# Two cross-attention layers on one core: the order of the second layer's heads, and its query channels with a batch in each of two PSUM banks

## The chip, the cores and the metric

The kernel runs on one core of a Trainium2 chip. The metric is the device time of one execution in microseconds (us), from the hardware's own clock; lower is better. The time before is the median of three runs. One further execution was profiled; durations of single instructions come from it.

## The reference

Two cross-attention layers follow each other. There are 64 batches of 256 tokens with 320 channels, and for each batch a context of 77 rows with 512 channels, of which the last 4 are image rows. All is fp32, with 20 heads of 16 channels. Cut to what matters:

```python
# layer 0                                  # layer 1
q = x @ Wq.T                               q = x1 @ W_q
p = softmax(q k^T / 4)     # 77 rows       p = softmax(q k_t^T / 4)    # 73 text rows
o = p v  (+ image part)                    t = p v_t
x1 = o @ Wo.T + bo + x                     sem = l2norm(p @ text) . l2norm(image rows)
                                           pi = softmax(q k_ip^T / 4 + 0.5 sem) * mask
                                           out = (t + pi v_ip) @ W_out + b_out + x1
```

Layer 1's input is layer 0's output, so layer 1 of a pair of batches can only start when layer 0 has finished with that pair.

## The kernel before, in words

Channels lie on partitions: 320 channels are two full tiles of 128 (`main`) and 64 left over (`last`). Two batches form a pair, and there are 32 pairs. The 64 left-over channels of a pair's first batch lie on partitions 0 to 63 and those of the second batch on partitions 64 to 127 of one tile, so `last` is a full 128-row tile with one batch in each half. The weights for it (`w[:, 2]` and `w[:, 3]`) have zeros in the other batch's half.

Heads go in three parts: part 0 and part 1 with eight heads each, part 2 with the last four. A unit is eight head-and-token-tile combinations: for parts 0 and 1 one half (128 tokens) of a batch's tokens, for part 2 four heads with both halves at once. `UNITS` lists the five units of a batch, so that a pair has `NU` = 10 units in each layer.

The main loop runs over blocks `g`; `p, k = divmod(g, NU)`, so ten blocks (k = 0 to 9) make a round. Block `g` handles unit `g` of layer 0 and unit `g - LAG` of layer 1, with `LAG` = 13: layer 1 of a pair begins in block 3 of the next round. In a block, in this order:

- TensorE computes into one four-bank tile `sc`: `semantics` of an earlier layer-1 unit (L762, L768), `scores` of layer 0, `scores` of layer 1 (L648).
- VectorE takes the maximum and subtracts it for both layers (`shifted`, L666 and L668), then multiplies the semantics with the probabilities (`weighted`, L779 and L782).
- TensorE transposes layer 1's probabilities of the previous block (`transposed`, L712 and L713), which ScalarE copies out (L719). ScalarE does layer 0's exponential (L676).
- Then comes the list `first` of extra steps, layer 0's transposes (L712; copies L738 and L739), `sums_out` (ScalarE, L1093), layer 1's exponential (L679, L680), `normalize` (L694, L695 on VectorE, L699 on POOL), what `later` holds, the list `second`, `attend` (L795, L800) and the list `third`.

`fillers(k, p)` says which extra steps stand in which block: projections of queries, keys and values, output projections, placing of values, and so on. The order on each engine is the order in which the program writes them (`keep_order`), so a waiting instruction holds all that is behind it on its engine.

PSUM has eight banks: four for `sc` (a single buffer), two for `ptr` (tag `tr`) and two for `pms` (tag `ms`). The next block's first matmul into `sc` needs this block's readers of it to be done, `sums_out` last.

The steps around the change:

- `queries(l, p, m)` makes query channels in one bank. For m = 0 and 1 it uses two matmuls of 512 columns over `main` (L562) and two of 256 columns over `last` (L564), whose stationary operand is 128 rows deep with one half zero; a copy (L565) follows. For m = 2, the last four heads, it uses four matmuls over `main` (L570) and four over `last` (L577), and a copy (L582).
- `halves(name, w, src)` makes 256 output channels with one batch in each of two banks: eight matmuls of 256 columns over `main` (L535), and later, in `rest()`, four over `last` (L544) that are 64 rows deep: batch 0 on rows 0 to 63, batch 1 on rows 64 to 127. `first_queries` uses it for layer 0's parts 0 and 1, and `project` for the output projections. Their ends are kept in `held` and are written at the start of the next block: the matmuls L544, then the drains (L593 on ScalarE for queries, four additions L608 on VectorE for a projection).
- `project_last` makes the last 64 output channels (L623) and adds them to the input tile (L627 on VectorE). After `project(0, p)` and `project_last(0, p)`, the input tile of pair `p` holds layer 1's input.
- The image attention of a batch runs through several blocks. Its exponential L925 (ScalarE) is in `later` of block 1 or 6, and `image_weights` (L932, L933 on VectorE) is in `early` of the next block, ahead of the drains.

Of the kernel before, what the change touches and what calls it, by code (L numbers as in the profile page):

```python
# [8 lines left out]
F32 = mybir.dt.float32  # L9
# [7 lines left out]
C = 320  # L17
E = 512
S = 256
# [3 lines left out]
P = 128  # L23
# [3 lines left out]
HALF = 64  # L27
# [4 lines left out]
QR = 32  # L32
SLOTS = H + 4

UNITS = ((0, 0), (0, 1), (1, 0), (1, 1), (2, 0))

PLACES = (0, 24, 8, 32, 16)
HT = H - 4
NU = 2 * len(UNITS)
LAG = NU + 3  # L40
SCALE = D**-0.5
SEM = 0.5
# [21 lines left out]
def tile_two_cross_attentions(ctx: ExitStack, tc: tile.TileContext, a: dict, out: bass.AP):  # L64
# [35 lines left out]
    nc = tc.nc  # L100
    x_in, c_in, cip_in = a["x"], a["ctx"], a["ctx_ip"]
    NB = x_in.shape[1] // S
    NP = NB // 2
    S2 = 2 * S
# [45 lines left out]
    cts, xts = {}, {}  # L150
# [400 lines left out]

    held = {}

    def queries(l, p, m):

        main, last = xts[p]
        ps = pms.tile([P, 512], F32, tag="ms", name=f"q_ps{l}_{p}_{m}")
        if m < 2:
            q = qs[l, p, m] = big.tile([P, S2], F32, tag=f"q{l}{m}", name=f"q{l}_{p}_{m}", bufs=1)
            c = slice(m * P, (m + 1) * P)  # L560
            for i in range(2):
                nc.tensor.matmul(ps, wq[l][:, i, c], main[:, i, :], start=(i == 0), stop=False)  # L562
            for b in range(2):
                nc.tensor.matmul(ps[:, b * S : (b + 1) * S], wq[l][:, 2 + b, c], last, start=False, stop=(b == 1))  # L564
            nc.scalar.copy(q, ps)  # L565
            return
        to = [ps[s * HALF : (s + 1) * HALF, :S].rearrange("p (b t) -> p b t", b=2) for s in range(2)]
        for i in range(2):
            for s in range(2):
                nc.tensor.matmul(  # L570
                    to[s], wq[l][:, i, C - HALF :],
                    main[:, i, :].rearrange("p (b s t) -> p b s t", b=2, s=2)[:, :, s, :],
                    start=(i == 0), stop=False,
                )
        for b in range(2):
            for s in range(2):
                nc.tensor.matmul(  # L577
                    to[s][:, b, :], wq[l][:, 2 + b, C - HALF :], last[:, s * P : (s + 1) * P],
                    start=False, stop=(b == 1),
                )  # L580
        q = qs[l, p, 2] = big.tile([P, 2, P], F32, tag=f"q{l}2", name=f"q{l}_{p}_2", bufs=1)
        nc.scalar.copy(q.rearrange("p b t -> p (b t)"), ps[:, :S])  # L582

    def first_queries(p):

        rest = halves(f"q_ps0_{p}", wq[0], xts[p])

        def end():
            ps = rest()
            q = big.tile([P, 2, S2], F32, tag="q0", name=f"q0_{p}")  # L590
            for m in range(2):
                qs[0, p, m] = q[:, m, :]
            return [lambda b=b: nc.scalar.copy(q[:, :, b * S : (b + 1) * S], ps[b]) for b in range(2)]  # L593

        held["q"] = end
# [45 lines left out]

    def scores(ps, start, stop, l, p, b, u):

        part, s = UNITS[u]
        q, kbd, t0 = qs[l, p, part], kbds[l, b], b * S + s * P
        for r in range(4):
            rows = slice(r * QR, (r + 1) * QR)
            nc.tensor.matmul(  # L648
                ps[:, r, 2 * T * l : 2 * T * (l + 1)], q[rows, b, :] if part == 2 else q[rows, t0 : t0 + P],
                kbd[rows, part].rearrange("p e t -> p (e t)"), start=start, stop=stop,  # L650
            )
# [52 lines left out]
    def transposed(l, p, b, u, w):  # L704

        n = P if l else 8 * R0
        part, s = UNITS[u]
        flat = w.rearrange("p i j t -> p (i j t)") if l else w
        ps = ptr.tile([P, 4, P], F32, tag="tr", name=f"tr{l}_{p}_{b}{u}")
        pr = ptr.tile([P, 4, P], F32, tag="tr", name=f"rtr{l}_{p}_{b}{u}")  # L710
        for i in range(4):
            nc.tensor.transpose(ps[:, i, :], flat[:, i * P : (i + 1) * P], ident)  # L712
        nc.tensor.transpose(pr[:n, 0, :], flat[:, 4 * P : 4 * P + n], ident)  # L713
        if l:
            pts[1] = (
                sp.tile([P, 4, P], F32, tag="pt1", name=f"pt1_{p}_{b}_{u}"),
                sp.tile([n, P], F32, tag="pr1", name=f"pr1_{p}_{b}_{u}"),
            )
            nc.scalar.copy(pts[1][0], ps)  # L719
            nc.scalar.copy(pts[1][1], pr[:n, 0, :])  # L720
            return
        if part == 2:
            pt, rt = pts[0, 2, b] = (
                sp.tile([P, 2, S], F32, tag="pt2", name=f"pt2_{p}_{b}"),
                sp.tile([n, P], F32, tag="pr2", name=f"pr2_{p}_{b}"),
            )
            nc.scalar.copy(
                pt.rearrange("p l (s t) -> p s l t", s=2), ps.rearrange("p (s l) t -> p s l t", s=2)
            )
            nc.scalar.copy(rt, pr[:n, 0, :])  # L730
            return
        if s == 0:
            pts[0, part] = (
                sp.tile([P, 4, S], F32, tag="pt0", name=f"pt0_{p}_{b}_{part}"),
                sp.tile([n, S], F32, tag="pr0", name=f"pr0_{p}_{b}_{part}"),
            )
        pt, rt = pts[0, part]
        nc.scalar.copy(pt[:, :, s * P : (s + 1) * P], ps)  # L738
        nc.scalar.copy(rt[:, s * P : (s + 1) * P], pr[:n, 0, :])  # L739
# [12 lines left out]
    def semantics(ps, start, stop, p, b, u, rows):  # L752

        part, _ = UNITS[u]
        pt, rt = rows
        for i in range(4):
            for j in range(2):
                half_rows = slice(j * M, (j + 1) * M)  # L760
                at = SEM0 + i // 2 * GV
                nc.tensor.matmul(  # L762
                    ps[:, i % 2 * 2 + j, at : at + GV], pt[half_rows, i, :], gv[b][half_rows, part, i, :],
                    start=start and i < 2, stop=False,
                )
        for r in range(4):
            quarter = slice(r * QR, (r + 1) * QR)
            nc.tensor.matmul(  # L768
                ps[:, r, SEM0 : SEM0 + 2 * GV].rearrange("p (e d) -> p e d", d=GV)[:, :, M:],
                rt[quarter, :], gr[b][quarter, part], start=False, stop=stop,  # L770
            )
# [13 lines left out]
    def attend(p, b, part):  # L785
# [2 lines left out]
        if (0, p) not in aTs:  # L788
            aTs[0, p] = channels("aT0", f"aT0_{p}", 1)
        main, last = aTs[0, p]  # L790
        ps = pms.tile([P, 2, S], F32, tag="ms", name=f"pv{p}_{b}_{part}")
        both = b == 1 and part == 1

        def heads(to, b, pair, pt, start):
# [186 lines left out]
    def fillers(k, p):  # L981
# [4 lines left out]
        def add(half, q, fn, *args):  # L986
            if 0 <= q < NP:
                f[half].append((fn, args))
# [12 lines left out]
        elif k == 1:  # L1001
            if p == 0:
                for l in range(2):
                    add(l, p, value_rows, 1, l)
                add(1, p, place_values, 0, p, 0)
            add(0, p, queries, 0, p, 2)
            add(1, p - 1, project, 0, p - 1)
            add(1, p - 2, last_image_values, p - 2, 0)
            add(1, p - 1, place_gram, 0)
            add(1, p, keys_by_head, 0, p, 1)  # L1010
# [1 line left out]
        elif k == 2:  # L1012
# [2 lines left out]
                    add(0, p, keys, 1, p, i)  # L1015
            add(0, p - 1, project_last, 0, p - 1)
            add(1, p + 1, load_x, p + 1)
            add(1, p - 1, queries, 1, p - 1, 0)
            add(1, p - 1, place_values, 1, p - 1, 0)
            add(1, p, values, 0, p, 1)  # L1020
        elif k == 3:
            add(0, p + 1, load_context, p + 1)
            add(0, p - 1, queries, 1, p - 1, 2)
            if p == 0:
                add(1, p, image_keys, 0)
            add(1, p - 1, queries, 1, p - 1, 1)
            add(1, p, place_values, 0, p, 1)
            add(1, p - 1, keys_by_head, 1, p - 1, 1)
        elif k == 4:
# [3 lines left out]
                add(0, p, keys, 1, p, 0)  # L1033
            add(1, p - 1, values, 1, p - 1, 1)
            add(1, p - 2, last_image_outputs, p - 2, 0)
            add(1, p + 1, first_queries, p + 1)
        elif k == 5:
            if p == 0:
                add(0, p, image_keys, 2)
# [39 lines left out]
    rows_todo, made_rows = [], [0, 1]  # L1079

    def unit(g):
        return (g // NU, g % NU // len(UNITS), g % len(UNITS)) if 0 <= g < NP * NU else None

    for i in range(2):
        keys(0, 0, i)
    last_keys(0)
    keys_by_head(0, 0, 0)
    first_queries(0)
    for fn in held.pop("q")():
        fn()  # L1090

# [7 lines left out]
    for g in range(NP * NU + LAG + 12):  # L1099
# [7 lines left out]
        for fn, args in early.pop(g, ()):  # L1107
            fn(*args)
        drains = [fn for what in ("q", "o") if what in held for fn in held.pop(what)()]
        if now[0] or now[1] or before1:  # L1110
            ps = psc.tile([P, 4, 512], F32, tag="sc", name=f"sc{g}")
            todo = []
            if before1:
                todo.append((semantics, (*before1[:3], before1[4])))
            for l in range(2):
                if now[l]:
                    todo.append((scores, (l, *now[l])))
            for n, (fn, args) in enumerate(todo):
                fn(ps, n == 0, n == len(todo) - 1, *args)
# [3 lines left out]
            drains += held.pop("i")()  # L1123
        for fn in drains:
            fn()
        ends = before1 and before1[2] == len(UNITS) - 1
        for l in range(2):
            if now[l]:
                shifted(ps, l, *now[l])
# [12 lines left out]
            keep_busy(6)  # L1142
        for fn, args in first:
            fn(*args)
        if before1 and k == 8:
            sums_out(ps)
        if last0:
            transposed(0, *last0)
# [6 lines left out]
            keep_busy(8)  # L1155
        if now[0] and k == 5:
            exponential(0, g, *now[0])
        if before1 and k != 8:
            sums_out(ps)
        if now[1]:  # L1160
            exponential(1, g, *now[1])
# [15 lines left out]
            fn(*args)  # L1177
        if last0:
            q, b, u, _ = last0
            if u == 1 or u == len(UNITS) - 1:  # L1180
                attend(q, b, int(u > 1))
        for fn, args in third:
            fn(*args)
# [58 lines left out]
```

## Time and profile before

| what | value |
|---|---|
| median of 3 runs | 2592.84 us (2590.41 to 2593.07) |
| the profiled execution | 2590.22 us |
| its span, first to last instruction | 2588.5 us |
| granted TensorE clock, mean | 0.998 |
| busy shares PE, DVE, ACT, POOL | 98%, 76%, 59%, 64% |
| first block with semantics starts | 113.05 us after the span's start |

Busy time is the time in which at least one instruction of an engine ran. PE is TensorE's matmuls, PEld its weight loads, DVE is VectorE, ACT is ScalarE, POOL is GpSimd. A busy share over the whole span is a mean over stages with different limits, so the stages that the change touches are read one by one, by the start times in the timeline. An arrow at the end of a timeline line names the idle time of the engine ahead of the group and who ended it.

### The profile page before, as it was taken

The numbers are of one execution on the slowest core, as the hardware profiler recorded it, in microseconds if no ns is written. First come the engines' busy times: TensorE is split into PE (matmuls) and PEld (weight loads), VectorE is DVE, ScalarE is ACT, GpSimd is POOL, SyncE is SP. The second block draws the span as 40 slices with busy tenths as digits, with TensorE's granted clock in tenths as the row PEclk, the third lists the DMA queues.
The fourth block names the chain that finished last, engine by engine and source line by source line (L and its number), as shares of the span: only waits on it lengthen the run. The fifth ranks groups of instructions, "written<-read, shape, count | busy, mean of one in ns | idle before, by whom it ended". The sixth has DMA issues, their size and how long they took to land.

```text
span 2588.5 us, 74021 instructions
## 1 busy us (share of the span) xinstructions
PE 2536.5 (98%) x26922; PEld 1977.1 (76%) x26922; DVE 1958.5 (76%) x3609; ACT 1520.3 (59%) x3893; POOL 1653.5 (64%) x4026
## 2 busy tenths in 40 slices
PE   7999999999999999999999999999999999999998
PEld 5677877777777777777777777777777777777676
DVE  4577777877777878777777777778777778777764
ACT  3465665665665665665665665665665665665543
POOL 3466666676666676666676666676666676666653
PEclk9999999999999999999999999999999999999999
DMA  5212211112211122211121211122211121211100
GB/s 165 59 44 59 65 45 44 51 54 60 62 47 48 47 59 55 62 45 49 48 59 55 62 45 50 47 59 54 64 44 50 45 60 54 62 40 40 27 25 26
DMA packets 186403, 138.29 MB, mean 53 GB/s; under 512 B 81017, under 2 KB 164729, under 8 KB 186041
## 3 DMA queue, kind: packets, MB, share of 16 engines
q1 hardware_dynamic: 185176, 132.41, 18.6%
q8 instruction: 215, 3.52, 0.6%
q14 instruction: 148, 1.20, 0.2%
q10 hardware_dynamic: 864, 1.15, 0.1%
HBM read 95.56 MB, written 33.91 MB: 50 GB/s over the span
## 4 chain that ended last, share of the span: by engine, by line
PE 89%; DVE 5%; ACT 2%; DMA 1%; POOL 1%; issue 1%; SPq 1%; DVEq 0%; ACTq 0%; POOLq 0%
PE sc L762 13%; PE tr L712 12%; PE o_ps L535 8%; PE sc L648 7%; PE sc L768 5%; PE v_ps L379 4%; PE q_ps L562 4%; PE q_ps L535 4%; PE k_ps L334 4%; PE o_ps L623 4%; PE pv L795 3%; PE o_ps L544 3%; PE pv L800 3%; PE q_ps L570 2%; PE rtr L713 2%; PE q_ps L564 2%
## 5 line engine op out<-in xcount | busy, mean ns | idle before, releaser
L666 DVE TENSOR_REDUCE mx<-sc 128x8 f32<-128x584 f32 (+1 forms) x640 | 497.5, 777 | 431.1 <-PE sc L648 431.0
L699 POOL TENSOR_TENSOR parts<-w,sm 128x512 f32<-128x512 f32 (+1 forms) x640 | 440.5, 710 | 372.3 <-DVE sm L695 163.7
L668 DVE TENSOR_TENSOR w<-sc,mx 128x616 f32<-128x616 f32 x640 | 512.0, 800 | 66.7 <-ACT kT L337 0.5
L719 ACT COPY pt<-tr 128x512 f32<-128x512 f32 x320 | 187.5, 586 | 466.4 <-PE tr L712 459.3
L712 PE MATMUL tr<-ident,parts 128*128 128x128 f32 x2560 | 410.1, 283 | 8.1 <-POOL parts L699 3.8
L762 PEld LDWEIGHTS sc<-gv,pt 64*128 64x128 f32 x5120 | 316.8, 187 | 88.2 <-ACT sums L1093 44.2
L712 PEld LDWEIGHTS tr<-ident,parts 128*128 128x128 f32 x2560 | 282.5, 141 | 117.8 <-issue 70.4
L762 PE MATMUL sc<-gv,pt 64*128 64x94 f32 x5120 | 356.3, 278 | 12.8 <-ACT sums L1093 10.4
L676 ACT ACTIVATE w<-w 128x616 f32<-128x616 f32 x320 | 231.0, 722 | 127.8 <-DVE w L668 119.2
L694 DVE TENSOR_REDUCE sm<-w 128x8 f32<-128x616 f32 x320 | 250.9, 784 | 14.4 <-ACT w L676 14.4
L648 PE MATMUL sc<-kbd,q 32*128 32x154 f32 x5120 | 247.6, 305 | 0.8 <-ACT q L593 0.8
L535 PE MATMUL o_ps<-aT,wo 128*128 128x256 f32 x1024 | 232.6, 380 | 0.0
L1168 DVE TENSOR_REDUCE nrm<-prod 128x8 f32<-128x584 f32 x320 | 227.0, 709 | 0.4
L779 DVE TENSOR_TENSOR prod<-sc,parts 128x512 f32<-128x512 f32 x320 | 217.9, 681 | 4.0 <-PE sc L768 4.0
L535 PEld LDWEIGHTS o_ps<-aT,wo 128*128 128x128 f32 x1024 | 190.4, 191 | 23.4
L679 ACT ACTIVATE parts<-w 128x512 f32<-128x512 f32 x320 | 206.9, 647 | 0.0
L738 ACT COPY pt<-tr 128x512 f32<-128x512 f32 x256 | 150.7, 589 | 69.7 <-PE tr L712 69.4
L648 PEld LDWEIGHTS sc<-kbd,q 32*128 32x128 f32 x5120 | 186.5, 186 | 5.4 <-issue 5.1
L1093 ACT COPY sums<-sc 128x168 f32<-128x168 f32 x320 | 96.6, 302 | 157.2 <-DVE prod L782 156.5
L683 POOL COPY att<-w 128x32 f32<-128x32 f32 x320 | 67.7, 212 | 186.9 <-DVE w L668 184.8
L379 PE MATMUL v_ps<-wv,cf 128*128 128x320 f32 (+1 forms) x624 | 182.1, 438 | 0.0
L713 PE MATMUL rtr<-ident,parts 128*104 128x128 f32 (+1 forms) x640 | 174.6, 273 | 0.0
(152 smaller groups left out, 4977.7 us busy)
## 6 DMA issues: line engine op xcount, KB each, us to landing
vip<-vip_rows SPq DMA_DIRECT2D x1024, 4.0 KB
out_dram<-x SPq DMA_DIRECT2D x64, 256.0 KB
x<-in_x_dram SPq DMA_DIRECT2D x31, 512.0 KB
v_rows<-vs SPq DMA_DIRECT2D x38, 320.0 KB
vm<-v_rows SPq DMA_DIRECT2D x152, 80.0 KB
ct<-in_ctx_dram SPq DMA_DIRECT2D x32, 308.0 KB
cf<-in_ctx_dram SPq DMA_DIRECT2D x38, 256.0 KB
g_rest<-gram_rest SPq DMA_DIRECT2D x512, 0.5 KB
```

Source lines behind the costliest of these rows:

```text
L379: nc.tensor.matmul(ps[:n, :C], cfs[i][:, k, :n], wv[l][:, k, :], start=(k == 0), stop=(k == KE - 1))
L535: nc.tensor.matmul(ps[b][:, m, :], w[:, k, m * P : (m + 1) * P], main[:, k, b * S : (b + 1) * S], start=(k == 0 and m == 0), stop=False,)
L648: nc.tensor.matmul(ps[:, r, 2 * T * l : 2 * T * (l + 1)], q[rows, b, :] if part == 2 else q[rows, t0 : t0 + P], kbd[rows, part].rearrange( ...
L666: nc.vector.tensor_reduce(mx, sc[:, :, :, :nt], AX.X, ALU.max)
L668: nc.vector.tensor_tensor(w, sc, mx.unsqueeze(3).broadcast_to([P, 4, 2, T]), ALU.subtract)
L676: nc.scalar.activation(w, w, AF.Exp, scale=SCALE)
L694: nc.vector.tensor_reduce(sm, w, AX.X, ALU.add)
L699: nc.gpsimd.tensor_tensor(two[:, 8 * t0 : 8 * t1].rearrange("p (h t) -> p h t", h=8), w[:, :, t0:t1], sm.unsqueeze(2).broadcast_to([P, 8, ...
L712: nc.tensor.transpose(ps[:, i, :], flat[:, i * P : (i + 1) * P], ident)
L713: nc.tensor.transpose(pr[:n, 0, :], flat[:, 4 * P : 4 * P + n], ident)
L762: nc.tensor.matmul(ps[:, i % 2 * 2 + j, at : at + GV], pt[half_rows, i, :], gv[b][half_rows, part, i, :], start=start and i < 2, stop=False,)
L1168: nc.vector.tensor_reduce(eight(stats[q, b][2], u), prod, AX.X, ALU.add)
```

## The change

Layer 1's list of units now begins with the last four heads. Its parts 0 and 1 are made by the two-bank form that layer 0 had, with their last contracted channels at the start of the next block. Some steps move for this. `queries(l, p)` replaces `first_queries(p)` and serves both layers; `last_queries(l, p)` makes the last four heads and returns its second half as a function of its own.

| block | before | after |
|---|---|---|
| 1 | `first`: layer 0's last-head queries; `second`: `project(0)` | `first`: `project(0)`; `sums_out` ahead of layer 0's transposes |
| 2 | `second`: layer 1's part 0 queries; `attend` in `ms` | `second`: first half of layer 1's last-head queries; `attend` in `tr` for batch 0, part 0; `third`: their second half |
| 3 | `first`: layer 1's last-head queries; `second`: layer 1's part 1 queries | `first`: layer 0's last-head queries; `second`: layer 1's parts 0 and 1 in two banks |
| 4 | | at its start: the rest of layer 1's parts 0 and 1, and two copies |

```diff
-UNITS = ((0, 0), (0, 1), (1, 0), (1, 1), (2, 0))
-PLACES = (0, 24, 8, 32, 16)
+UNITS = (((0, 0), (0, 1), (1, 0), (1, 1), (2, 0)), ((2, 0), (0, 0), (0, 1), (1, 0), (1, 1)))
+BU = len(UNITS[0])
+PLACES = (16, 0, 24, 8, 32)
...
-    def queries(l, p, m):
+    def last_queries(l, p):
         main, last = xts[p]
-        ps = pms.tile([P, 512], F32, tag="ms", name=f"q_ps{l}_{p}_{m}")
-        if m < 2:
-            q = qs[l, p, m] = big.tile([P, S2], F32, tag=f"q{l}{m}", name=f"q{l}_{p}_{m}", bufs=1)
-            c = slice(m * P, (m + 1) * P)
-            for i in range(2):
-                nc.tensor.matmul(ps, wq[l][:, i, c], main[:, i, :], start=(i == 0), stop=False)
-            for b in range(2):
-                nc.tensor.matmul(ps[:, b * S : (b + 1) * S], wq[l][:, 2 + b, c], last, start=False, stop=(b == 1))
-            nc.scalar.copy(q, ps)
-            return
+        ps = pms.tile([P, 512], F32, tag="ms", name=f"q_ps{l}_{p}_2")
...
-        for b in range(2):
-            for s in range(2):
-                nc.tensor.matmul(
...
+        def rest():
+            for b in range(2):
+                for s in range(2):
+                    nc.tensor.matmul(
...
+        return rest
+
+    def queries(l, p):
+        rest = halves(f"q_ps{l}_{p}", wq[l], xts[p])
         def end():
             ps = rest()
-            q = big.tile([P, 2, S2], F32, tag="q0", name=f"q0_{p}")
+            q = big.tile([P, 2, S2], F32, tag=f"q{l}", name=f"q{l}_{p}", bufs=2 - l)
             for m in range(2):
-                qs[0, p, m] = q[:, m, :]
+                qs[l, p, m] = q[:, m, :]
...
-        ps = pms.tile([P, 2, S], F32, tag="ms", name=f"pv{p}_{b}_{part}")
+        pool, tag = (pms, "ms") if b or part else (ptr, "tr")
+        ps = pool.tile([P, 2, S], F32, tag=tag, name=f"pv{p}_{b}_{part}")
...
-            add(0, p, queries, 0, p, 2)
-            add(1, p - 1, project, 0, p - 1)
+            add(0, p - 1, project, 0, p - 1)
...
-            add(1, p - 1, queries, 1, p - 1, 0)
+            add(1, p - 1, lambda: made.update(q=last_queries(1, p - 1)))
+            add(2, p - 1, lambda: made["q"]())
...
-            add(0, p - 1, queries, 1, p - 1, 2)
+            add(0, p, lambda: last_queries(0, p)())
...
-            add(1, p - 1, queries, 1, p - 1, 1)
+            add(1, p - 1, queries, 1, p - 1)
...
         drains = [fn for what in ("q", "o") if what in held for fn in held.pop(what)()]
+        for fn in drains:
+            fn()
+        drains = []
...
-        if before1 and k == 8:
+        if before1 and k in (1, 8):
             sums_out(ps)
...
-        if before1 and k != 8:
+        if before1 and k not in (1, 8):
             sums_out(ps)
```

The scores of layer 1 in block 4 now read what the drains at that block's start write; so the drains are written ahead of the scores, in every block.

## The prediction

> **What bounds the kernel now.** I read the page first (busy shares, then the chain that ended last), then TensorE's timeline over one round of ten blocks in mid-run, then the windows of single blocks, then VectorE's and ScalarE's timelines there.
>
> Page of the kernel before, parts 1 and 4:
>
> ```profile
> PE 2536.5 (98%) x26922; PEld 1977.1 (76%) x26922; DVE 1958.5 (76%) x3609; ACT 1520.3 (59%) x3893; POOL 1653.5 (64%) x4026
> ...
> PE 89%; DVE 5%; ACT 2%; DMA 1%; POOL 1%; issue 1%; SPq 1%; DVEq 0%; ACTq 0%; POOLq 0%
> ```
>
> TensorE is busy all the time and carries the chain. Next, blocks 1, 2 and 3 of round 17, each from one first semantics matmul (L762) to the next (window; length, busy us by engine):
>
> ```profile
> 1314.93:1324.22 9.29, 9.29 (x92) 7.63 (x93) 7.26 (x15) 4.65 (x14) 6.37 (x12) 1.00 0.08 18
> 1324.22:1332.73 8.51, 8.51 (x88) 5.24 (x84) 7.39 (x14) 3.80 (x9) 5.09 (x12) 1.00 0.42 116
> 1332.73:1340.18 7.45, 7.45 (x78) 5.23 (x75) 5.02 (x9) 3.78 (x10) 3.79 (x18) 1.00 0.14 36
> ```
>
> In all three, PE (second figure) is busy for the whole block and the granted clock is 1.00. These lengths repeat within 0.01 us from round to round. So in these blocks a TensorE microsecond saved is a microsecond of the span, as long as nothing else becomes late. Only the 0.33 us before block 7 (L762 waiting for the sums copy L1093) is a regular idle gap, and the change does not touch it.
>
> TensorE's timeline (start, us, groups; "xN" counts two records for each fp32 matmul):
>
> ```profile
> 1328.88 1.88 PE L562 MATMUL q_ps<-x,wq 128*128 128x512 f32 x4
> 1330.67 1.13 PE L564 MATMUL q_ps<-x,wq 128*128 128x256 f32 x4
> 1331.73 0.64 PE L795 MATMUL pv<-pt,v 128*32 128x256 f32 x8
> ...
> 1337.50 1.88 PE L562 MATMUL q_ps<-x,wq 128*128 128x512 f32 x4
> 1339.22 1.03 PE L564 MATMUL q_ps<-x,wq 128*128 128x256 f32 x4
> 1340.18 1.13 PE L762 MATMUL sc<-gv,pt 64*128 64x94 f32 x16
> ...
> 1344.35 3.62 PE L535 MATMUL q_ps<-x,wq 128*128 128x256 f32 x16
> 1347.90 1.14 PE L544 MATMUL q_ps<-x,wq 64*128 64x256 f32 x8
> 1348.87 1.03 PE L762 MATMUL sc<-gv,pt 64*128 64x94 f32 x16
> ```
>
> Ends are modelled, so I count from start to start. The two old layer-1 query steps take 1331.73 - 1328.88 = 2.85 and 1340.18 - 1337.50 = 2.68, together 5.53 us. The last three lines are layer 0's queries, already in the form (`halves`) that the change gives layer 1: 3.55 + 0.97 = 4.52 us. Same columns, but the two batches' last 64 channels stand in the two halves of the rows and run side by side.
>
> **The sum on TensorE alone**, for one round:
> - Block 1 loses layer 0's last-head queries (L570 at 1317.64 to the transposes at 1319.10: 1.46). Project then lies before the transposes, as in block 9, which needs 7.82 with that order: 9.29 to 7.82 or a little less, -1.47.
> - Block 2 loses L562 and L564 (2.85) and gains layer 1's last-head queries in two pieces (0.92 + 0.54 = 1.46): 8.51 to 7.12, -1.39.
> - Block 3 swaps layer 1's last-head queries for layer 0's (same cost), and its second step (2.68) for the whole two-bank form (4.52): 7.45 to 9.29, +1.84.
> - Together -1.02, which is 5.53 - 4.52 again.
>
> The Trainium skill ("TensorEngine Tiling (Array Packing)", Key Properties) says that a change of tiling mode drains TensorE, which speaks against 64-row pieces. Here the drain is in the row already: L535 to L544 is 3.55, against 3.46 from project's sixteen L535 records to transposes; and the semantics behind it are 64-row too, so no switch is added. By the rule the sum would stay.
>
> **What becomes late next.** Block 1 shrinks, but some work between blocks 1 and 2 does not follow TensorE. ScalarE and VectorE there, before:
>
> ```profile
> 1305.81 0.59 ACT L738 COPY pt<-tr 128x512 f32<-128x512 f32 x1 [2.04 <-PE tr L712]
> ...
> 1322.28 0.33 ACT L925 ACTIVATE num<-num 128x160 f32<-128x160 f32 x1
> ```
>
> ```profile
> 1322.84 0.31 DVE L932 TENSOR_REDUCE imx<-num 128x40 f32<-128x160 f32 x1
> 1323.18 0.40 DVE L933 RECIPROCAL imx<-imx 128x40 f32<-128x40 f32 x1
> 1324.42 1.66 DVE L608 SCALAR_TENSOR_TENSOR x<-o_ps,bo,x 128x256 f32<-128x256 f32 x4 [0.83 <-PE o_ps L544]
> 1326.27 0.80 DVE L666 TENSOR_REDUCE mx<-sc 128x8 f32<-128x616 f32 x1 [0.19 <-PE sc L648]
> ...
> 1330.14 0.47 DVE L627 SCALAR_TENSOR_TENSOR x<-o_ps,bo,x 128x256 f32<-128x256 f32 x1
> ```
>
> The first of these is block 9's copy after late transposes. In block 1 the transposes of layer 0 now come after project. I count from block 1's start:
> - The copy L738 starts at 6.72 (block 9: 1305.81 - 1299.09). Before, it started at 4.86. The sums copy moved ahead of it costs nothing: it may start at 6.46 (when VectorE's product is done, as before) and takes 0.20 of queue.
> - Behind L738 on ScalarE, by the steps of block 9: L739 7.20, L679 7.36, L680 7.90; then the image exponential L925, 0.15 later as before, 8.05 to 8.38. Before it ended at 7.68.
> - VectorE's queue puts L932 and L933, which read it, ahead of project's four additions L608. L932 starts at about 8.45, L933 0.34 later, L608 another 0.31 later (as between L830 and L608 in block 0): 9.10. TensorE would have had project ready at about 7.9.
> - L608 to the first maximum L666 is 1.48 (block 0: 1308.34 to 1309.82): 10.58. From there to the end of L627 is 1330.61 - 1326.27 = 4.34: 14.92.
> - L627 writes the last channels of layer 1's input. The second piece of layer 1's last-head queries (L577) reads them. L564 read them before, 0.05 after L627's end, so that wait already held the path by some 0.1 to 0.2 (2.85 against 2.68).
>
> TensorE would reach L577 at 7.75 + 6.58 = 14.3, and now waits until 14.97. With 0.54 for the piece and some 0.1 for weights that could not be loaded ahead, block 3 starts at 15.6, not at 14.9. On the way the attention step L795 also waits some 0.3 for copies that follow the late VectorE; that is covered by the same end. Behind the waiting L577 on TensorE stand block 3's semantics and scores, and so everybody. Blocks 1 and 2 thus take 15.6 where they took 17.80, -2.2; block 3 gives back 1.84. **Net: -0.38 us a round**, not -1.02.
>
> **What costs nothing, and its cover.** In block 4 the first layer-1 scores wait for the two query copies (L593, 1.06 for both); the semantics and layer-0 scores ahead of them last 1.68 and ScalarE is free there (its last exponential ended 0.3 before L565 in the old block 3). If that cover goes, see the fourth case. The last-head copy (L582, 0.35) has the same 1.68 at block 3. The attention step in the other bank pair follows copies that are waited for anyway. Drains written ahead of the scores keep each engine's order. Layer 0's last heads, moved to block 3, are read in block 4. No DMA moves against another on SP. Reordering layer 1's heads changes no size; its last-head keys (L365) were placed 5.6 before block 3 and, with POOL unchanged, still are over 2 before it.
>
> **Total.** Thirty-one rounds hold both layers; the first has no layer 1, the 33rd no layer 0 and is filled with spare transposes, so I count neither (a microsecond or so each way; the start waits for DMAs and POOL around the moved 1.46). 31 x 0.38 = 11.8. The profiled execution took 2590.22 (span 2588.5, 1.7 around it): 2578.4. The runs' median, 2592.84, lies 2.6 higher, so I give 2581 for the median.
>
> **The cases.**
> 1. Chain as above, 0.6. My steps may be off by 0.2 in all, so net -0.2 to -0.6 a round: 2574 to 2587.
> 2. No new wait, 0.22: 31 x 1.02 = 31.6, 2561. For it: VectorE idles 0.83 before L608 and 2.72 in block 3, so half a microsecond somewhere in my steps would remove most of the wait. Against it: L925's place behind L680 and L932's ahead of L608 are fixed orders.
> 3. Nothing gained, 0.1: the wait grows by 0.4 more (VectorE's spans stretch, L577's weights are late); 2588 to 2598. The Trainium skill ("Perfetto Trace Analysis", Identifying the Most-Contended Engine) calls matmul busy share a poor measure and the share of weight loads a better one; that is 76% here, so by it TensorE has room and freed time would be waited away, as in this case. Against it stand block lengths that equal the sum of their matmul steps.
> 4. Slower, 0.08: the copies L593 in block 4. In block 5 before, two table loads kept them until 1350.38, 1.51 after the block's start. If ScalarE were as late in block 4, the layer-1 scores would start at about 2.65 instead of 1.68: +0.97 a round, on top of -0.38: +18, 2611. It decides from a ScalarE delay of 0.6. Against it: the table loads come at the ends of blocks 9 and 4 only, not 3.
>
> That the saving isn't there at all (the pieces not running side by side) is ruled out by layer 0's 0.97.
>
> **Range and chances.** Case 1 and most of case 2, with the upper edge just into case 3: 2561 to 2590. A measurement here can tell about 0.2%, or 5 us, from no change. Faster 0.80, within 0.12, slower 0.08.
>
> **What the new profile would show.** Layer 1's queries as sixteen and eight records, 4.5 us from start to start; block 1 at 7.7 to 7.8, block 3 at 9.3; L608 of block 2 starting 1.3 after its block and not 0.2; TensorE idle before L577, released by L627, 0.4 to 0.7 in each round. No idle there means case 2; idle at layer-1 scores of block 4, released by the copies, case 4. I am wrong if VectorE reaches L608 at 0.2 as before, or if another wait appears in blocks 4 to 9, which I took as unchanged.

## The result, and the profile after

| | before | changed |
|---|---|---|
| median | 2592.84 us (5 runs, 2590.41 to 2594.01) | 2581.55 us (5 runs, 2578.30 to 2586.83) |
| profiled execution | 2590.22 us | 2582.37 us |

The ratio is 0.996, with a 95% interval of 0.9945 to 0.9975: faster, by more than a measurement here can blur. The forecast was 2581. The net came out this close partly by chance: terms that I had missed go in both directions, and the experiments show them.

The page of the changed kernel:

```profile
PE 2514.9 (97%) x27178; PEld 2010.2 (78%) x27178; DVE 1954.0 (76%) x3609; ACT 1510.1 (59%) x3893; POOL 1653.7 (64%) x4026
...
PE 68%; DVE 16%; ACT 4%; POOL 3%; DMA 3%; SPq 3%; issue 3%; DVEq 0%; POOLq 0%; ACTq 0%
```

TensorE's busy time fell by 21.6 us, the span only by 7.9 (2588.5 to 2580.6). The chain that ended last now runs through VectorE for 16% instead of 5%: part of the freed time became a wait. The windows of blocks 1, 2 and 3 of the same round:

```profile
1306.88:1314.57 7.69, 7.69 (x76) 6.71 (x77) 6.33 (x13) 3.66 (x11) 4.77 (x10) 1.00 0.03 6
1314.57:1322.47 7.90, 7.55 (x96) 4.79 (x92) 7.30 (x15) 3.81 (x12) 5.69 (x13) 1.00 0.47 132
1322.47:1331.76 9.29, 9.29 (x92) 7.63 (x92) 6.23 (x12) 3.94 (x11) 6.63 (x20) 1.00 0.15 36
```

The second figure is PE again: in block 2 it is 0.35 short of the block's length. TensorE's timeline names the place:

```profile
1319.39 1.08 PE L564 MATMUL q_ps<-x,wq 128*64 128x256 f32 x8
1320.46 0.64 PE L794 MATMUL pv<-pt,v 128*32 128x256 f32 x8
1320.92 0.62 PE L799 MATMUL pv<-pr,vr 104*32 104x256 f32 x8
1321.88 0.66 PE L573 MATMUL q_ps<-x,wq 128*64 128x128 f32 x8 [0.35 <-DVE x L625]
1322.47 1.13 PE L760 MATMUL sc<-gv,pt 64*128 64x94 f32 x16
...
1327.24 3.62 PE L537 MATMUL q_ps<-x,wq 128*128 128x256 f32 x16
1330.79 1.13 PE L546 MATMUL q_ps<-x,wq 64*128 64x256 f32 x8
1331.76 1.03 PE L760 MATMUL sc<-gv,pt 64*128 64x94 f32 x16
```

(The changed file has other line numbers. Matmuls: L537 is what L535 was, L546 is L544, L564 is L570 and not the old L564, L573 is L577, L760 is L762, L766 is L768, L794 is L795, L799 is L800. Others: L606 is L608, L625 is L627, L736 is L738, L924 is L925, L931 is L932.) The last three lines are layer 1's queries in the new form, 3.55 + 0.97 = 4.52. The wait list has this wait before L573 30 times, 10.5 us in all. ScalarE's and VectorE's lines around it are the chain that I had laid out:

```profile
1313.60 0.59 ACT L736 COPY pt<-tr 128x512 f32<-128x512 f32 x1
...
1314.93 0.33 ACT L924 ACTIVATE num<-num 128x160 f32<-128x160 f32 x1
```

```profile
1315.30 0.32 DVE L931 TENSOR_REDUCE imx<-num 128x40 f32<-128x160 f32 x1 [0.42 <-ACT num L924]
1315.65 0.40 DVE L932 RECIPROCAL imx<-imx 128x40 f32<-128x40 f32 x1
1315.97 1.61 DVE L606 SCALAR_TENSOR_TENSOR x<-o_ps,bo,x 128x256 f32<-128x256 f32 x4
...
1321.36 0.47 DVE L625 SCALAR_TENSOR_TENSOR x<-o_ps,bo,x 128x256 f32<-128x256 f32 x1
```

Counted from block 1's start (1306.88), the copy is at 6.72, the image exponential at 8.05, the image reduction at 8.42, project's additions at 9.09, the end of L625 at 14.95, L573 at 15.00 and block 3 at 15.59.

Median lengths of blocks, rounds 4 to 30 (the difference between neighbouring first semantics matmuls in the trace):

| block | before | forecast | after |
|---|---|---|---|
| 1 | 9.29 | 7.7 to 7.8 | 7.69 |
| 2 | 8.51 | 7.8 to 7.9 | 7.91 |
| 3 | 7.45 | 9.29 | 9.29 |
| 4 | 8.69 | 8.69 | 8.58 |
| sum | 33.94 | 33.56 | 33.47 |

The medians of blocks 0 and 5 to 9 moved by less than 0.02. That is 0.47 us a round, 14.6 for 31 rounds. The profiled run gained 7.85 only, so something outside the median rounds gave some 7 back; the last two experiments are about that.

### The profile page after: what moved, and what is told of

It is laid out like the page before. It is cut to its first block, busy times and chain, and to the rows that moved or that the text cites. A ratio compares the mean times of both kernels' runs of the same rounds, so it can differ in the third digit from the quotient of the medians.

```text
span 2580.6 us, 74528 instructions
## 1 busy us (share of the span) xinstructions
PE 2514.9 (97%) x27178; PEld 2010.2 (78%) x27178; DVE 1954.0 (76%) x3609; ACT 1510.1 (59%) x3893; POOL 1653.7 (64%) x4026
## 4 chain that ended last, share of the span: by engine, by line
PE 68%; DVE 16%; ACT 4%; POOL 3%; DMA 3%; SPq 3%; issue 3%; DVEq 0%; POOLq 0%; ACTq 0%
PE sc L760 10%; PE q_ps L537 8%; PE tr L710 8%; PE sc L646 6%; DVE w L666 5%; PE v_ps L381 4%; DVE mx L664 4%; PE o_ps L537 4%; PE sc L766 4%; PE k_ps L336 4%; PE q_ps L546 3%; DVE prod L777 2%; PE pv L794 2%; DVE x L606 2%; PE pv L799 2%
## 5 line engine op out<-in xcount | busy, mean ns | idle before, releaser
L760 PEld LDWEIGHTS sc<-gv,pt 64*128 64x128 f32 x5120 | 319.5, 187 | 71.9 <-ACT sums L1092 44.1
L760 PE MATMUL sc<-gv,pt 64*128 64x94 f32 x5120 | 353.1, 277 | 12.8 <-ACT sums L1092 10.3
L537 PE MATMUL q_ps<-x,wq 128*128 128x256 f32 x1024 | 233.5, 381 | 3.3 <-ACT kT L339 3.3
L537 PE MATMUL o_ps<-aT,wo 128*128 128x256 f32 x1024 | 232.6, 380 | 0.0
L537 PEld LDWEIGHTS q_ps<-x,wq 128*128 128x128 f32 x1024 | 190.0, 191 | 27.6 <-ACT kT L339 4.3
L537 PEld LDWEIGHTS o_ps<-aT,wo 128*128 128x128 f32 x1024 | 190.3, 191 | 23.5 <-issue 0.2
L736 ACT COPY pt<-tr 128x512 f32<-128x512 f32 x256 | 150.1, 586 | 63.0 <-PE tr L710 62.7
```

The costliest lines, as they stand in the source:

```text
L537: nc.tensor.matmul(ps[b][:, m, :], w[:, k, m * P : (m + 1) * P], main[:, k, b * S : (b + 1) * S], start=(k == 0 and m == 0), stop=False,)
L760: nc.tensor.matmul(ps[:, i % 2 * 2 + j, at : at + GV], pt[half_rows, i, :], gv[b][half_rows, part, i, :], start=start and i < 2, stop=False,)
```

## The experiments

My theory (A): TensorE bounds the rounds, the two batches' last channels run side by side and save 1.0 us a round, and half of it is lost in block 2 because two small VectorE steps of the image attention wait for a late ScalarE exponential and stand ahead of project's additions. The rival (B): VectorE is simply full in blocks 1 and 2, and the order of its queue does not matter. A third reading is that the gain has nothing to do with the row halves. All kernels below are the changed kernel with the edit shown; the ratio in brackets is against the kernel before, measured alongside, with its 95% interval.

**1. The image weights behind the normalization** (`imgw_later`)

```diff
-                early[g + 3] = [(image_weights, (q, b))]
+                (early if b else later)[g + 3] = [(image_weights, (q, b))]
```

> The image weights of a pair's first batch (a reduction and a reciprocal on VectorE, 0.65 us) move from the start of block 2, ahead of project's four additions, to behind the normalization of block 2. Theory A (VectorE's queue: these two wait for a late ScalarE exponential and hold the additions): the additions start about 8.0 us after block 1's start instead of 9.1, the 0.35 idle before L573 goes, block 2 takes 7.1 to 7.2 instead of 7.91, 31 rounds x 0.75 = 23 us less, about 2558. Rival B (VectorE is simply full: 14.65 us busy in blocks 1 and 2 before, against 15.6 that they now take): order within its queue does not matter much, 2575 to 2582.

Measured: 2566.96 us (0.9902, 0.9887 to 0.9917). Block 2 of its trace (TensorE):

```profile
1314.70 1.08 PE L564 MATMUL q_ps<-x,wq 128*64 128x256 f32 x8
1315.71 0.64 PE L794 MATMUL pv<-pt,v 128*32 128x256 f32 x8
1316.17 0.62 PE L799 MATMUL pv<-pr,vr 104*32 104x256 f32 x8
1316.72 0.66 PE L573 MATMUL q_ps<-x,wq 128*64 128x128 f32 x8
1317.31 1.13 PE L760 MATMUL sc<-gv,pt 64*128 64x94 f32 x16
```

The wait before L573 is gone, and block 2 takes 7.36 in every round instead of 7.91. B falls: VectorE has the room, its queue stood in the wrong order. The gain is 0.55 a round and not the 0.75 that I expected of it, because TensorE alone needs 7.36 here and not the 7.12 of my sum. The 0.24 lie where the shape of TensorE's tile changes (the shape is the figure ahead of the operands). After the transposes the 64-column piece L564 starts 0.20 behind the last one, where a 128-column piece started 0.11 behind it (1337.39 to 1337.50 before). L564 to the 32-column L794 takes 1.01, where L570 to L577 of one shape took 0.91. And L573 stands behind another shape again. At these places the trace also shows the later piece's weights loaded only when it starts (PEld and PE of L564 both at 1314.70, of L573 both at 1316.72), where within one shape they were loaded ahead (L577 before: weights at 1336.15, matmuls at 1336.36).

**2. The same two steps, only just behind the additions** (`imgw_behind`)

```diff
-        for fn, args in early.pop(g, ()):
-            fn(*args)
         drains = [fn for what in ("q", "o") if what in held for fn in held.pop(what)()]
         for fn in drains:
             fn()
+        for fn, args in early.pop(g, ()):
+            fn(*args)
```

> The same two VectorE steps only change places with the four additions at the start of block 2. Theory A: additions at about 8.0, but the two steps still lie ahead of block 2's first maximum, which then starts at about 10.2 after block 1's start instead of 10.62; block 2 about 7.5, 31 x 0.4 = 12 us less, about 2569. Rival B: 2575 to 2582.

Measured: 2566.66 us (0.9899, 0.9884 to 0.9913), the same as the first. VectorE:

```profile
1308.03 1.65 DVE L606 SCALAR_TENSOR_TENSOR x<-o_ps,bo,x 128x256 f32<-128x256 f32 x4
1309.59 0.31 DVE L931 TENSOR_REDUCE imx<-num 128x40 f32<-128x160 f32 x1
1309.94 0.40 DVE L932 RECIPROCAL imx<-imx 128x40 f32<-128x40 f32 x1
1310.26 0.74 DVE L664 TENSOR_REDUCE mx<-sc 128x8 f32<-128x616 f32 x1
```

Block 1 of this round starts at 1300.12: the additions are at 7.91 and the first maximum at 10.14, as expected (8.0 and 10.2). Block 2 has a median of 7.38. Here the two steps still use VectorE ahead of the maximum; what is gone is the waiting for ScalarE, and that is enough, since TensorE's own 7.36 now ends last. I expected 2569 because I still took 7.12 for that.

**3. 128 rows instead of 64 for the last channels** (`rows128`)

```diff
-                    rows = slice(b * HALF, (b + 1) * HALF)
+                    rows = slice(0, P) if deep else slice(b * HALF, (b + 1) * HALF)
...
+        rest = halves(f"q_ps{l}_{p}", wq[l], xts[p], deep=l == 1)
```

> As the changed kernel, but the last contracted channels of layer 1's 256 query channels are 128 rows deep (weights with zeros in the other batch's half) instead of 64 rows per batch. Same results, same places. Theory A (the gain on TensorE is the two batches running side by side): four matmuls of 256 columns in a row, 4 x 0.45 = 1.8 instead of 0.97 from start to start, 31 rounds x 0.85 = 26 us more, about 2608. Rival (the gain comes from the new order of steps, not from the row halves): no change, 2578 to 2587.

Measured: 2605.11 us (1.0048, 1.0031 to 1.0065). TensorE at the end of block 3:

```profile
1346.42 1.89 PE L546 MATMUL q_ps<-x,wq 128*128 128x256 f32 x8
1348.24 1.13 PE L760 MATMUL sc<-gv,pt 64*128 64x94 f32 x16
1349.31 0.45 PE L766 MATMUL sc<-gr,pr 32*128 32x60 f32 x8
```

The same eight records take 1.82 from start to start instead of 0.97. Block 3 is 10.05 instead of 9.29. Block 4 is 8.68 instead of 8.58: its semantics take 1.07 from L760 to L766 behind a 128-row piece, and 0.96 behind a 64-row piece (1331.76 to 1332.72 in the changed kernel), whose tile shape they share. That is the 0.11 of block 4 that I had not counted. The shape alone does not decide it: in block 0 of the kernel before, the semantics stand behind the 64-row L544 too and take 1.07 (1306.90 to 1307.97). What goes with the 0.11 in all three is the first weight load: 0.21 ahead of the matmuls in the changed block 4 (1331.55), with them in `rows128` (1348.24) and only 0.03 ahead in block 0 (1306.87), where it came late. Without the row halves, the new order alone is slower than the kernel before. The total rose by 23.6 us and not by 31 x 0.86 = 26.7, because block 4 had fewer late rounds here (experiment 7).

**4. The sums copy back behind the transposes' copies in block 1** (`sums_late`)

```diff
-        if before1 and k in (1, 8):
+        if before1 and k == 8:
...
-        if before1 and k not in (1, 8):
+        if before1 and k != 8:
```

> As the changed kernel, but in block 1 the sums copy stands behind the copies of layer 0's transposes again. Theory A: it pushes layer 1's exponentials and so the image exponential by 0.2, and with them the chain through VectorE to L573: blocks 1 and 2 take 15.8 instead of 15.6, block 1 alone 7.8; 31 x 0.2 = 6 us more, about 2588. Rival: only block 2's start moves (0.1) and the wait before L573 takes it up, no change.

Measured: 2586.89 us (0.9977, 0.9968 to 0.9987). Blocks 1 and 2 have medians of 7.73 and 8.07, together 0.20 more than in the changed kernel: a 0.2 us step on ScalarE, several links away, arrives whole at TensorE. The totals differ by 5.3, though the two intervals overlap; the block lengths are the firmer evidence.

**5. The attention step in its old bank pool** (`pv_ms`)

```diff
-        pool, tag = (pms, "ms") if b or part else (ptr, "tr")
-        ps = pool.tile([P, 2, S], F32, tag=tag, name=f"pv{p}_{b}_{part}")
+        ps = pms.tile([P, 2, S], F32, tag="ms", name=f"pv{p}_{b}_{part}")
```

> As the changed kernel, but the attention step of batch 0, part 0 (block 2) takes its bank from the pool ms again, as before the change. Theory A (block 2 ends with VectorE's chain): of the two ms banks one holds the open last-head queries and the other is free only when L625 has read project's last channels, 14.95 after block 1's start; so the attention step (1.0) starts there instead of ahead of it, and the second half of the last-head queries behind it: block 2 takes 8.9 instead of 7.91, 31 x 1.0 = 31 us more, about 2612. Rival (banks are free in time, the place is indifferent): 2578 to 2587.

Measured: 2611.21 us (1.0078, 1.0063 to 1.0093).

```profile
1339.68 0.64 PE L793 MATMUL pv<-pt,v 128*32 128x256 f32 x8 [1.50 <-DVE x L625]
1340.11 0.64 PE L798 MATMUL pv<-pr,vr 104*32 104x256 f32 x8
1340.69 0.66 PE L573 MATMUL q_ps<-x,wq 128*64 128x128 f32 x8
```

The wait is now 1.50 and sits before the attention step, released by the same VectorE instruction; block 2 takes 9.00. This small line of the change is worth 1.1 us a round, more than the whole net gain of 0.47.

**6. Both VectorE moves together** (`best`): the edit of the first experiment, and the image maximum L920 behind the product.

```diff
-        if g in middle:
-            fn, args = middle.pop(g)
-            fn(*args)
...
             prod = weighted(ps, *before1[:4])
+        if g in middle:
+            fn, args = middle.pop(g)
+            fn(*args)
```

> The changed kernel with the image weights of the first batch behind the normalization of block 2 (as in imgw_later, 2566.96) and the image maximum L920 (0.31 us on VectorE, blocks 1 and 6) behind the product with the semantics instead of ahead of it. Theory: in block 6 the sums copy waits for that product, and block 7's first matmul waits 0.33 for the sums copy; with 0.23 of queue taken away from ahead of the product the wait falls to 0.1: about 0.2 in most rounds, 6 us less than imgw_later, 2561. Rival (the maximum is then too late for the image exponential, which holds ScalarE): no gain or a loss, 2566 to 2575.

Measured: 2561.26 us (0.9889, 0.9872 to 0.9905). Block 6 falls from 6.82 to 6.59, and the wait at block 7 from 0.33 to 0.11. Block lengths settle what the total alone would not, since the interval touches that of the first experiment.

**7 and 8. Two buffers for the value rows** (`vm2`, and `best_vm2` with the edits of 6)

The changed kernel's wait list has a line that grew, and a place in round 25 shows what it does (POOL waiting for a load of value rows; then TensorE):

```profile
POOL v L455 <- DMA vm<-v_rows: 27.9, 10, 6.5
```

```profile
1953.90 1.89 PE L537 MATMUL q_ps<-x,wq 128*128 128x256 f32 x8
1958.42 3.28 PE L537 MATMUL q_ps<-x,wq 128*128 128x256 f32 x8 [2.63 <-ACT kT L339]
1961.63 1.49 PE L546 MATMUL q_ps<-x,wq 64*128 64x256 f32 x8
```

Before, the same line read 8.8 us, 7 times, 2.0 at the longest. In round 25, POOL starts the placing 6.5 late, so the keys by head behind it, so the key copy on ScalarE, and TensorE idles for 2.63. Then eight records take 3.21 instead of about 1.8: the granted clock was one half from 1959.0 for 3.4 us. Block 4 of that round took 13.11.

```diff
-        vm = small.tile([P, C], F32, tag="vm", name=f"vm{l}_{p}_{b}", bufs=1)
+        vm = small.tile([P, C], F32, tag="vm", name=f"vm{l}_{p}_{b}", bufs=2)
...
-        num = nums[p, b] = small.tile(full, F32, tag="num", name=f"num{p}_{b}", bufs=2)
+        num = nums[p, b] = small.tile(full, F32, tag="num", name=f"num{p}_{b}", bufs=1)
```

> The changed kernel with two buffers instead of one for the value rows vm (and one instead of two for the image scores num, to make room). In the profiled run of the changed kernel block 4 was longer than usual in rounds 17, 20 and 25, by 0.2, 0.96 and 4.54 us, because POOL waited for vm; in round 25 the clock was halved for 3.4 us after that. Theory C (the one buffer is free only when layer 1's values have been placed in block 2, so the load for block 3's placing starts too late once the round is shorter): these waits go, about 5 to 6 us less, 2576. Rival D (the load is late on its queue, behind other transfers, whatever the buffer): the same waits, 2578 to 2587.

> The same two buffer counts on top of the kernel best (image weights and image maximum moved), whose profiled run had block 4 longer by 6.7 us in all, over seven rounds. Theory C: about 6 us less than best's 2561.3, 2555. Rival D: 2558 to 2565.

Measured: `vm2` 2576.61 us (0.9947, 0.9934 to 0.9961), `best_vm2` 2555.09 us (0.9864, 0.9851 to 0.9878).

```profile
POOL v L455 <- DMA vm<-v_rows: 3.2, 2, 2.8
```

That is the wait list of `vm2`. In both traces block 4 is 8.58 to 8.59 in all rounds from 4 to 30, and no half clock lies in mid-run. So these waits need the one buffer, and D falls. Why the load of round 25 was so slow stays open: its last issue ended at 1947.95 and POOL waited until 1955.73, where in round 17 an issue that ended at 1328.74 was in time for 1331.06. In totals the interval of each kernel overlaps that of its partner with one buffer. Both medians fall by 5 to 6 us, but the kernel before was 2.5 us faster too when `vm2` was measured (2590.37), so for `vm2` the traces carry the verdict. `best_vm2` is the fastest of all: 1.4% under the kernel before.

The buffer is not all of the 7 us. Over rounds 4 to 30, block 4 lost 5.8 in the changed kernel and 1.1 in the kernel before, which makes 4.7. Another 2.7 went in block 5 of rounds 31 and 32 (9.59 and 8.32, before 8.46 and 6.77): there the clock was at one half for 3.4 us each, from 2426.6 and 2498.3, right behind waits of 1.53 and 1.60. The kernel before and `vm2` have waits of the same lengths there (1.53, and 1.60 and 1.59) at a clock of 1.00.

## Why the prediction was right, and where it was not

- **What bounds the kernel**: right. TensorE's freed time arrived wherever nothing else was late, and 0.85 us added to it (experiment 3) arrived whole in the lengths of blocks 3 and 4 (0.76 and 0.10).
- **TensorE's sum**: the total, -1.02 a round, stands (with the wait gone in `imgw_later`, blocks 1 to 4 are 7.69 + 7.36 + 9.29 + 8.58 = 32.92, against 33.94), but by luck, since its parts do not. Block 2 without a wait is 7.36, not 7.12: the sum priced the split last-head queries at 0.92 + 0.54 and left out that the tile's shape changes more often around them. Block 1 came out 0.13 under the 7.82 of block 9, and block 4 lost 0.11 because its semantics now follow a piece of their own shape and their weights are loaded ahead. The three errors, +0.24, -0.13 and -0.11, cancel.
- **The tiling rule**: I wrote that no switch is added, and that by the rule the sum would stay. The trace contradicts that reading: at the changes of shape above, about 0.1 us was lost for every piece that moved, not only for the 64-row ones. The Trainium skill ("TensorEngine Tiling (Array Packing)", Key Properties) says that a change of mode drains TensorE. Whether the 0.1 is that drain or the late weight load seen at the same places, no run here separates; block 0 lost it without a change of shape.
- **The chain through ScalarE and VectorE**: right, link by link, within 0.05 us. Experiments 1, 2 and 4 confirm its order and the 0.2 step in it.
- **The size of the wait**: 0.35 at L573, where I had 0.67, since TensorE got there later than I thought. The attention step ahead of it lost about 0.06 to its late copies (1.07 from L564 to L794, against 1.01 in `imgw_later`), not 0.3. The end of block 2 is set by VectorE, so its start of block 3 (15.59 against 15.6) did not depend on that.
- **Costs at nothing**: right for the sums copy, the query copies in block 4 (1.0 us of waiting for them in the whole run) and the other bank. That last one has a large price if left out.
- **Blocks 4 to 9 unchanged**: wrong. The load of value rows has one buffer, and in a few rounds it came too late for block 4; that gave back about 5 us. That the shorter rounds are the reason is not shown: in `rows128` the rounds are longer than before (76.65 before, 77.05 there, as sums of the blocks' medians), and block 4 of its round 25 was still 1.9 longer than usual.
- **The total**: -0.38 a round was -0.47. (The terms as I printed them, 15.6 - 17.80 + 1.84, make -0.36.) Block 4's 0.11 is the gain that I had missed, 3.4 us over 31 rounds; the late loads (4.7) and the half clock in rounds 31 and 32 (2.7) are the losses. So the profiled execution took 2582.37, 4.0 more than the 2578.4 that I had for it. I then added 2.6 because the median before lay that far above its profiled execution; the changed kernel's median lies 0.8 below its own. A median within 1 us of the forecast is therefore chance in part. Without late loads and half clock, `vm2` shows the 14.6 in its profiled execution: 2574.64, 15.6 under 2590.22, of which 1.1 are the late loads of the kernel before.

## What to carry to other kernels

When an engine that is busy all the time gets a microsecond back, follow the other engines' queues through the same stage, step by step from measured starts. Here a reduction and a reciprocal, 0.65 us together, queued ahead of work that the bound engine needs, cost half of the gain. Look also at single-buffered loads: here one was late in a few rounds only, which a typical round does not show.

## What was not expected of the hardware

- The same semantics take 0.96 us where their first weights were loaded 0.21 ahead, and 1.07 where they were not, be it behind a piece of another tile shape (`rows128`) or behind one of their own (block 0 of the kernel before).
- One idle stretch of 2.63 us was followed by 3.4 us at half the clock, so a late transfer was paid for twice: 2.63 of idle time, and about 1.8 more for the matmuls behind it (3.21 instead of about 1.8 for L537, 1.32 instead of 0.97 for L546), of the 13.11 - 8.58 = 4.53 in all. Waits of 1.53 and 1.60 us in rounds 31 and 32 were followed by it too, but not in `vm2`, so the length of a wait does not decide alone. The three stretches start at 1959.0, 2426.6 and 2498.3, 137 and 21 times 3.413 us apart; where a wait falls against such a grid may decide, which no run here tests. The Trainium skill ("TensorE: Matmul & The Clock Gate", Part 1: The HAM clock gate) says that the clock halves after at least one idle window of about 3.4 us and comes back after a busy window of about that length. The 3.4 us at half the clock agree with the second; for the first, waits of less than half that length were enough here.
